# Graph attention by three sums with 0/1 fp32r patterns as stationary operands and weighted tables as moving ones

## The chip, the cores and the metric

The kernel runs on one NeuronCore of a Trainium2 chip. The metric is the device time of one execution in microseconds, as the median over the runs. One execution was also profiled; every share and duration below is of that one. The engines are called as in the profile: PE is TensorE (PEld its weight loads), DVE is VectorE, ACT is ScalarE, POOL is GpSimd, and SP issues most of the DMAs.

## The reference

Four graph layers over N = 2708 nodes with 512 features and one 0/1 adjacency matrix `adj` (about 2.4% ones, symmetric, ones on the diagonal). Each layer normalizes its input, applies a relu, and adds its result to x. Layers 0, 1 and 3 multiply the adjacency (or a part of it) by features. Layer 2, the one that changes, is attention with 8 heads of 64 outputs:

```python
Wh = jnp.einsum('nd,hdo->hno', x, W)
f1 = jnp.einsum('hno,ho->hn', Wh, a1)
f2 = jnp.einsum('hno,ho->hn', Wh, a2)
e = jax.nn.leaky_relu(f1[:, :, None] + f2[:, None, :], negative_slope=0.2)
e = jnp.where(adj[None, :, :] > 0, e, NEG_INF)
attention = jax.nn.softmax(e, axis=-1)
h_prime = jnp.einsum('hnm,hmo->hno', attention, Wh)
out = jax.nn.elu(h_prime)
```

Since leaky_relu is max(s, 0.2 s), the weight of a pair is max(exp(f1+f2), exp(0.2(f1+f2))); a factor that depends on the row alone falls out of the softmax.

## The kernel before

`fast_layers` does the four layers one after the other. Nodes are cut into NC = 22 chunks of R = 126 (the last has 62), and the chunks into six groups of 4, 4, 4, 4, 3, 3. The transposed adjacency stays in SBUF as int8 tiles `vT`, written in layer 0; `pattern(m, cs)` is its block of row chunk m and column chunks cs. The residual x lives in DRAM between the layers (x1, x2, x3).

Layers 1, 2 and 3 each begin with a dense part: `staged` runs, chunk by chunk and each stage one step behind the other, load, `norm` (statistics on DVE, a square root on ACT), `relu_T` (four PE transposes, the relu copy `hT` on ACT) and the products. Layers 0, 1 and 3 then call an aggregation: for every group and every row chunk, DVE makes a 0/1 block of fp32r (`kt`, L539 and L763) and PE multiplies it, as stationary operand, with two parts of the features (`halves`, L306), 512 columns each.

The dense part of layer 2 (`product2`) also gives f1 and f2 for each node, in `f12`; `row2` writes f1 transposed to DRAM (`rT`). After it DVE works out `bad` and a matmul the verdict that decides whether the fast path holds, and the fused weights of layer 3 are loaded. Then comes the attention, for three spans of 7, 8 and 7 column chunks, in each for eight heads: SP loads a row of rT to all partitions (`rb`), ACT takes its exponential. For each of 22 row chunks ACT multiplies it by a scalar per partition (L717), DVE takes the maximum with another scalar and multiplies with the pattern (L720), and PE multiplies with Wh as stationary operand, 65 columns wide (64 outputs and a column of ones), in fp32 with two banks of 504 or 378 moving columns (L730). An fp32 matmul is two PE instructions in the profile. `finish` transposes the result back, divides, applies the elu and adds the residual on POOL (L697).

[...]

## Time and profile before

| | |
|---|---|
| median of 3 runs (lowest, highest) | 2176.9 us (2171.16, 2180.18) |
| profiled execution: own time | 2177.88 us |
| its span, first to last instruction | 2176.0 us |
| mean granted PE clock | 0.987 |
| PE busy | 2096.1 us, 7162 instructions |
| DVE busy | 1394.2 us, 2155 instructions |
| ACT busy | 988.2 us, 1506 instructions |
| POOL busy | 245.7 us, 419 instructions |
| DMA moved | 140.65 MB, mean 65 GB/s |

The stages are told apart by the first and last PE instruction of each line:

| stage | us from the span's start |
|---|---|
| layer 0, with the fusion of layer 3's weights | 0 to 414.4 |
| layer 1, dense | 414.4 to 584.8 |
| layer 1, aggregation | 584.8 to 805.8 |
| layer 2, dense and verdict | 805.8 to 929.1 |
| layer 2, attention | 929.1 to 1787.0 |
| layer 3, dense | 1787.0 to 1948.1 |
| layer 3, aggregation | 1948.1 to 2176.0 |

A group's line names the line of the source, the engine, the operation, the tile written and those read, the shape, the count; after the bar come busy time in us and mean length of one in ns; after the second bar the idle time of the engine in front of them, with what ended it. In the timeline, instructions of one group that follow each other are merged: start, length from the first start to the last end, and the count.

### The profile page before, as it was taken

How to read it: one execution, taken by the hardware profiler on the slowest of the kernel's cores; microseconds unless marked ns; L12 is line 12 of the kernel's file. 1: busy time of each engine (PE TensorE's matmuls, PEld its weight loads, DVE VectorE, ACT ScalarE, POOL GpSimd, SP SyncE). 2: the span in 40 equal slices, each digit the busy share in tenths (PEclk: the TensorE clock that was granted, in tenths of full speed). 3: DMA queues.
4: the chain of work that ended last, by engine and by line, in shares of the span. 5: the costliest groups of instructions: out<-in, count | busy, mean ns of one | idle time of the engine just before them, and what ended most of it. 6: DMA issues, size and time to landing. Idle time of an engine off the chain costs nothing.

```text
span 2176.0 us, 21201 instructions
## 1 busy us (share of the span) xinstructions
PE 2096.1 (96%) x7162; PEld 1101.0 (51%) x7162; DVE 1394.2 (64%) x2155; ACT 988.2 (45%) x1506; POOL 245.7 (11%) x419
## 2 busy tenths in 40 slices
PE   8999998899999989799999999999999999999998
PEld 4556666544588764333333333333333334458886
DVE  5556778644455667677888787878887864323343
ACT  3456787611100002277777777767777752210000
POOL 1002323211111212300000000000010100000000
PEclk9999999999999999999999999999999999999999
DMA  7324544322311222110101110100110003211131
GB/s 241 89 76 143 147 144 143 104 68 76 103 39 39 74 68 65 37 33 26 25 25 34 54 29 28 29 19 25 31 32 25 24 12 99 68 50 58 58 112 35
DMA packets 118230, 140.65 MB, mean 65 GB/s; under 512 B 57128, under 2 KB 73748, under 8 KB 118112
## 3 DMA queue, kind: packets, MB, share of 16 engines
q1 hardware_dynamic: 80008, 103.74, 16.3%
q10 hardware_dynamic: 37528, 33.37, 5.0%
q0 software_dynamic: 576, 2.10, 0.3%
q8 instruction: 58, 0.95, 0.2%
q14 instruction: 60, 0.49, 0.1%
HBM read 103.54 MB, written 35.46 MB: 64 GB/s over the span
## 4 chain that ended last, share of the span: by engine, by line
PE 50%; ACT 3%; DMA 2%; DVE 2%; issue 1%; POOL 0%; SPq 0%; ACTq 0%; DVEq 0%; POOLq 0%
PE att L730 32%; PE acc L306 10%; PE nb_ps L165 3%; PE self_ps L165 3%; ACT t L717 2%; DMA rb<-rT 2%; DVE t L720 1%; PE out_ps L666 1%; ACT ot L663 1%; PE hT_ps L186 0%; DVE ln_st L170 0%; ACT rb L709 0%; POOL xs L697 0%; DVE x L775 0%; DVE hn L177 0%
## 5 line engine op out<-in xcount | busy, mean ns | idle before, releaser
L730 PE MATMUL att<-t,wh 126*65 126x504 f32 (+2 forms) x2112 | 832.8, 555 | 9.2 <-DVE t L720 9.2
L720 DVE SCALAR_TENSOR_TENSOR t<-t,eg,vT 126x882 f32<-126x882 f32 (+3 forms) x528 | 631.5, 1210 | 165.6 <-ACT t L717 156.4
L717 ACT ACTIVATE t<-rb,ef 126x882 f32<-126x882 f32 (+3 forms) x528 | 554.7, 1063 | 217.4 <-PE att L730 172.7
L730 PEld LDWEIGHTS att<-t,wh 126*65 126x65 f32 (+1 forms) x2112 | 288.6, 138 | 537.4 <-issue 450.0
L306 PE MATMUL acc<-halves,kt 126*126 126x512 f32 x1848 | 432.3, 395 | 0.0
L306 PEld LDWEIGHTS acc<-halves,kt 126*126 126x126 f32 x1848 | 344.0, 186 | 86.3 <-issue 1.0
L306 PE MATMUL acc<-halves,ar 126*126 126x512 f32 x924 | 254.9, 416 | 4.7 <-DVE ar L387 3.9
L306 PEld LDWEIGHTS acc<-halves,ar 126*126 126x126 f32 x924 | 166.1, 189 | 48.6 <-issue 7.0
L174 ACT ACTIVATE ln_rs<-ln_mv,eps 126x1 f32<-126x1 f32 x88 | 25.3, 294 | 306.3 <-DMA x<-x 208.7
L539 DVE SCALAR_TENSOR_TENSOR kt<-lastr,index,vT 126x504 fp32r<-126x504 int16 (+1 forms) x132 | 104.3, 798 | 83.2 <-PE acc L306 83.0
L697 POOL TENSOR_TENSOR xs<-xs,e 126x448 f32<-126x448 f32 (+3 forms) x32 | 53.6, 1686 | 822.1 <-DVE e L683 822.1
L763 DVE CAST kt<-vT 126x504 fp32r<-126x504 int8 (+1 forms) x132 | 52.7, 400 | 144.8 <-PE acc L306 140.8
L394 DVE TENSOR_TENSOR_SCAN cum<-ai,deg 126x504 int16<-126x504 int32 (+2 forms) x110 | 124.7, 1140 | 24.1 <-DMA ai<-in_adj 14.9
L404 ACT ACTIVATE sign<-cum,limit 126x504 bf16<-126x504 int16 (+3 forms) x132 | 88.5, 670 | 69.3 <-DVE cum L394 62.2
L188 ACT ACTIVATE hT<-hT_ps 128x504 f32<-128x504 f32 x88 | 51.2, 587 | 148.9 <-PE hT_ps L186 126.3
L170 DVE BATCH_NORM_STATS2 ln_st<-x 126x6 f32<-126x512 f32 x88 | 60.0, 684 | 74.3 <-DMA x<-x 67.3
L165 PE MATMUL wh_ps<-w2s,hT 128*126 128x512 f32 (+1 forms) x176 | 83.3, 617 | 9.2 <-ACT hT L188 9.2
L444 ACT CAST vT<-vT_ps 126x504 int8<-126x504 f32 (+1 forms) x132 | 70.7, 537 | 46.4 <-DVE sums L435 23.8
L389 ACT ACTIVATE ab<-ai 126x504 bf16<-126x504 int32 (+3 forms) x132 | 76.1, 579 | 18.3 <-DMA ai<-in_adj 12.9
L165 PE MATMUL nb_ps<-wn,hT 128*126 128x512 f32 x176 | 81.5, 607 | 2.6 <-ACT hT L188 2.6
L165 PE MATMUL h_ps<-w0s,hT 128*126 128x512 f32 x176 | 79.3, 593 | 0.2 <-ACT hT L188 0.2
L165 PE MATMUL nb_ps<-wfn,hT 128*126 128x512 f32 x176 | 79.3, 593 | 0.2 <-ACT hT L188 0.2
(135 smaller groups left out, 1535.8 us busy)
## 6 DMA issues: line engine op xcount, KB each, us to landing
x<-x SPq DMA_DIRECT2D x105, 252.0 KB
ai<-in_adj SPq DMA_DIRECT2D x84, 248.1 KB
x<-x ACTq DMA_DIRECT2D x63, 252.0 KB
x<-in_x SPq DMA_DIRECT2D x42, 252.0 KB
rb<-rT SPq DMA_DIRECT2D x16, 434.1 KB
s<-y ACTq DMA_DIRECT2D x21, 252.0 KB
sc<-s SPq DMA_DIRECT2D x21, 252.0 KB
out_x<-x ACTq DMA_DIRECT2D x21, 252.0 KB
```

The lines of the kernel that those rows point to most:

```text
L165: nc.tensor.matmul(po[:n], lhsT[:, f, :n], w[:, f, :], start=(f == 0), stop=(f == NF - 1))
L170: nc.vector.bn_stats(st[:n], xc[:n])
L306: nc.tensor.matmul(acc[:R], weight[:, k * R : (k + 1) * R], parts[:, i, :], start=(m == 0 and i == 0), stop=(m == NC - 1),)
L389: nc.scalar.activation(ab[:n, :gw], ai[:n, :gw], AF.Square)
L394: nc.vector.tensor_tensor_scan(cum[:n, :gw], ai[:n, :gw], ai[:n, :gw], 0.0 if g == 0 else deg[:n, m : m + 1], op0=ALU.add, op1=ALU.max,)
L404: nc.scalar.activation(sign[:n, :gw], cum[:n, :gw], AF.Sign, bias=limit[:n], scale=-1.0, accum_out=signs[:n, m, g : g + 1],)
L444: nc.scalar.copy(vT[g][:, :, m * R : (m + 1) * R], pt[:R, :K, :R])
L539: nc.vector.scalar_tensor_tensor(by_chunk(kt, cs), lastr[:, cs[0] * R : (cs[-1] + 1) * R].rearrange("p (c r) -> p c r", r=R), index[:R, m ...
L697: nc.gpsimd.tensor_tensor(xs[:n, :q], xs[:n, :q], e[:n, k : k + q], ALU.add)
L717: nc.scalar.activation(t[:n, :W], rb[:n, :W], AF.Copy, scale=ef[:n, m, hd : hd + 1])
L720: nc.vector.scalar_tensor_tensor(by_chunk(t, cs)[:n], by_chunk(t, cs)[:n], eg[:n, m, hd : hd + 1], pattern(m, cs, n), op0=ALU.max, op1=ALU ...
L730: nc.tensor.matmul(a[:O1, : hi - lo], wh[:n, m, hd, :], t[:n, lo:hi], start=(m == 0), stop=(m == NC - 1),)
```

## The change

The weight max(A, B) of a pair is A where f1 + f2 > 0 and B elsewhere. So the sum over neighbours is split into three: the sum of exp(f2) Wh over the neighbours with f2 > -f1, the sum of exp(0.2 f2) Wh over the same ones, and the sum of exp(0.2 f2) Wh over all neighbours, from which the second is taken away. The patterns hold 0 and 1 in fp32r; the weighted Wh is kept as an fp32r part and the remainder, also in fp32r.

- The dense part of layer 2 stores Wh (with its column of ones) to DRAM (`whd`). For the first pair of heads it also builds the tables: the exponentials on ACT (`tables2`), the products on POOL (`build_product`), the first part as a copy on ACT (`build_first`), the remainder on POOL (`build_second`). A table covers two row chunks and two heads; 14 buffers hold the 11 of a pair of heads and three to spare. Tables of the other pairs are built during the attention, from Wh loaded back (`load_pair`).
- The attention runs over 4 pairs of heads, 4 spans of 6, 6, 5, 5 column chunks and the 2 heads: 32 units of 22 steps. At each step DVE makes one fp32r mask (`make_mask`, five buffers, four steps ahead), and PE multiplies each 126 columns of it, as stationary operand, with 260 columns of a table. The sums over all neighbours are made once for a pair of heads: ACT casts blocks of the pattern to fp32r (`make_block`), PE multiplies them (`multiply_adj`) in between by a count (`fill`), nine steps of it at each change of unit.
- After a unit ACT copies the sums from PSUM, with a factor per row for one of them (`evict`). POOL subtracts and adds (`sum_up`), DVE takes the reciprocal and POOL multiplies (`divide`), ACT and DVE do the elu, and POOL adds the residual, loaded by SP (`load_res`), for two heads at a time (`store`).
- The verdict is worked out after the dense part of layer 3, the maxima of w2 within layer 1's aggregation.
- The pools `common` and `ps` are closed before the attention and opened again after it; they and those of the attention and layer 3 wait for reused memory tile by tile (`reuse_waits="tile"`). Several pools move to the right side of SBUF.

```diff
-    common = ctx.enter_context(tc.tile_pool(name="common", bufs=2))
-    ps = ctx.enter_context(tc.tile_pool(name="ps", bufs=8, space=PSUM))
+    def open_front():
+        nonlocal front, common, ps
+        front = ctx.enter_context(ExitStack())
+        common = front.enter_context(tc.tile_pool(name="common", bufs=2, reuse_waits="tile"))
+        ps = front.enter_context(tc.tile_pool(name="ps", bufs=8, space=PSUM, reuse_waits="tile"))
+    front = common = ps = None
+    open_front()
...
+    HP = H // 2
+    W1 = 2 * O1
+    l2 = ExitStack()
+    wk = l2.enter_context(tc.tile_pool(name="l2", bufs=1, side="right"))
+    whd = dram.tile([NC * R, H * O1], F32, name="whd")
+    scales = wk.tile([R, HP, NC, 4], F32, name="scales")
+    u = wk.tile([R, NC, H], F32, name="u")
+    def build_product(p, i, parts):
+        raw = wk.tile([R, 2, 4, O1], F32, name="raw", bufs=2)
+        for k, src in parts:
+            q = src.shape[1] // 2
+            nc.gpsimd.tensor_tensor(
+                raw[:, k : k + q].rearrange("p m (h e) o -> p (m h) e o", e=2),
+                src.unsqueeze(2).to_broadcast([R, 2 * q, 2, O1]),
+                scales[:, p, 2 * i + k : 2 * i + k + q, :]
+                .rearrange("p m (h e) -> p (m h) e", e=2)
+                .unsqueeze(3)
+                .to_broadcast([R, 2 * q, 2, O1]),
+                ALU.mult,
+            )
+        built[p, i] = raw
+    def build_first(p, i):
+        t = wk.tile([R, 2, 4, 2, O1], F32R, name="table", bufs=RING)
+        nc.scalar.copy(
+            t[:, :, :, 0, :].rearrange("p m e o -> p (m e) o"),
+            built[p, i].rearrange("p m e o -> p (m e) o"),
+        )
+        tables[p, i] = t
+    def build_second(p, i, eng):
+        t = tables[p, i]
+        v = t.rearrange("p m e q o -> p (m e) q o")
+        eng.tensor_tensor(
+            v[:, :, 1, :],
+            built.pop((p, i)).rearrange("p m e o -> p (m e) o"),
+            v[:, :, 0, :].bitcast(F32),
+            ALU.subtract,
+        )
+        tables[p, i] = t.rearrange("p m e q o -> p m (e q o)")
...
+            wh = whs[c % 4]
+            nc.scalar.copy(wh[:n, :, :O], po[:n].rearrange("p (h o) -> p h o", h=H))
+            nc.sync.dma_start(whd[c * R : (c + 1) * R, :], wh.rearrange("p h o -> p (h o)"))
...
+        def tables2(c):
+            if c % 2 == 0:
+                return
+            f2 = f12[:R, c - 1 : c + 1, H:].rearrange("p c (h e) -> p c h e", e=2)
+            for e, scale in ((slice(0, 4, 3), 1.0), (slice(1, 3), SLOPE2)):
+                nc.scalar.activation(
+                    scales[:, :, c - 1 : c + 1, e].rearrange("p h c e -> p c h e"),
+                    f2,
+                    AF.Exp,
+                    scale=scale,
+                )
+            build_product(0, c // 2, [(k, whs[(c - 1 + k) % 4][:, :2, :]) for k in range(2)])
+        def first2(c):
+            if c % 2:
+                build_first(0, c // 2)
+                build_second(0, c // 2, nc.gpsimd)
+        staged(
+            NC, *dense(x2, product2, False, [(5, row2), (5, tables2), (6, first2)])
+        )
+        nc.scalar.activation(u, f12[:R, :, :H], AF.Exp, scale=1.0 - SLOPE2)
+    front.close()
...
+    sizes2 = [6, 6, 5, 5]
+    spans = [list(range(sum(sizes2[:g]), sum(sizes2[: g + 1]))) for g in range(len(sizes2))]
+    SM = max(sizes2)
+    wide = [(p, cs) for p in range(HP) for cs in spans]
+    units = [(p, cs, e) for p, cs in wide for e in range(2)]
+    UNITS = len(units)
+    PIECE = 2
+    pieces = [
+        (t, k, cs[k : k + PIECE]) for t, (p, cs) in enumerate(wide) for k in range(0, len(cs), PIECE)
+    ]
+    blocks = [(j, g) for j in range(len(pieces)) for g in range(len(groups))]
...
+        at = stack.enter_context(tc.tile_pool(name="att", bufs=1, reuse_waits="tile"))
+        pe = stack.enter_context(tc.tile_pool(name="pe", bufs=3, space=PSUM, reuse_waits="tile"))
+        pg = stack.enter_context(tc.tile_pool(name="pg", bufs=1, space=PSUM, reuse_waits="tile"))
...
+        def make_mask(i):
+            n, m = divmod(i, NC)
+            p, cs, e = units[n]
+            q = rows(m)
+            mask[i] = at.tile([R, SM * R], F32R, name="mask", bufs=5)
+            nc.vector.scalar_tensor_tensor(
+                by_chunk(mask[i], cs)[:q],
+                by_chunk(row[n], cs)[:q],
+                f12[:q, m, H + 2 * p + e : H + 2 * p + e + 1],
+                pattern(m, cs, q),
+                op0=ALU.is_lt,
+                op1=ALU.mult,
+            )
+        def multiply(i):
+            n, m = divmod(i, NC)
+            p, cs, e = units[n]
+            q = rows(m)
+            if m == 0:
+                acc[n] = [
+                    pe.tile([P, 2, 512], F32, name="acc2") for _ in range(0, len(cs), 2)
+                ]
+            for k in range(len(cs)):
+                nc.tensor.matmul(
+                    acc[n][k // 2][:R, k % 2, : 2 * W1],
+                    mask[i][:q, k * R : (k + 1) * R],
+                    tables[p, m // 2][:q, m % 2, 2 * e * W1 : 2 * (e + 1) * W1],
+                    start=(m == 0),
+                    stop=(m == NC - 1),
+                )
+        def evict(n):
+            p, cs, e = units[n]
+            t = at.tile([R, SM, 2, 2, O1], F32, name=f"sums{e}")
+            flat = t.rearrange("p c g q o -> p c g (q o)")
+            for k, c in enumerate(cs):
+                a = acc[n][k // 2]
+                nc.scalar.activation(
+                    flat[:, k, 0],
+                    a[:R, k % 2, e * W1 : (e + 1) * W1],
+                    AF.Copy,
+                    scale=u[:, c, 2 * p + e : 2 * p + e + 1],
+                )
...
+            sums[n] = t
+        def make_block(b):
+            j, g = blocks[b]
+            cs = pieces[j][2]
+            K = len(groups[g])
+            block[b] = at.tile([R, KMAX, PIECE * R], F32R, name="block", bufs=3)
+            nc.scalar.copy(
+                block[b][:, :K, : len(cs) * R], vT[g][:, :, cs[0] * R : (cs[-1] + 1) * R]
+            )
...
+        def multiply_adj(i):
+            j, m = divmod(i, NC)
+            t, k0, cs = pieces[j]
+            p, _ = wide[t]
+            q = rows(m)
+            g, gk = where[m]
+            b = j * len(groups) + g
...
+            if m == 0:
+                accg[j] = pg.tile([P, PIECE, 512], F32, name="accg")
+            for k in range(len(cs)):
+                nc.tensor.matmul(
+                    accg[j][:R, k, : 2 * W1],
+                    block[b][:q, gk, k * R : (k + 1) * R],
+                    tables[p, m // 2][:q, m % 2, W1 : 3 * W1],
+                    start=(m == 0),
+                    stop=(m == NC - 1),
+                )
+            if m == NC - 1:
+                if k0 == 0:
+                    whole[t] = at.tile([R, SM, 2, 2, O1], F32, name="whole")
+                nc.scalar.copy(
+                    whole[t].rearrange("p c h q o -> p c (h q o)")[:, k0 : k0 + len(cs)],
+                    accg.pop(j)[:R, : len(cs), : 2 * W1],
+                )
...
+        def sum_up(t):
+            p, cs = wide[t]
+            y[t] = at.tile([R, SM, 2, O1], F32, name="y2")
+            parts[t] = [(k, min(3, len(cs) - k)) for k in range(0, len(cs), 3)]
+            for e in range(2):
+                s = sums[2 * t + e].rearrange("p c g q o -> p c g (q o)")
+                w = whole[t].rearrange("p c h q o -> p c h (q o)")
+                for k, q in parts[t]:
+                    v = slice(k, k + q)
+                    nc.gpsimd.tensor_tensor(s[:, v, 1], w[:, v, e], s[:, v, 1], ALU.subtract)
+            for e in range(2):
+                s = sums[2 * t + e].rearrange("p c g q o -> p c g (q o)")
+                for k, q in parts[t]:
+                    v = slice(k, k + q)
+                    nc.gpsimd.tensor_tensor(s[:, v, 0], s[:, v, 0], s[:, v, 1], ALU.add)
+            for e in range(2):
+                s = sums.pop(2 * t + e)
+                for k, q in parts[t]:
+                    v = slice(k, k + q)
+                    nc.gpsimd.tensor_tensor(y[t][:, v, e], s[:, v, 0, 0], s[:, v, 0, 1], ALU.add)
...
+        def divide(t):
+            p, cs = wide[t]
+            K = len(cs)
+            rs = at.tile([R, SM, 2, 1], F32, name="rs2", bufs=2)
+            nc.vector.tensor_scalar(rs[:, :K], y[t][:, :K, :, O:], TINY, None, op0=ALU.max)
+            nc.vector.reciprocal(rs[:, :K], rs[:, :K])
+            for k, q in parts[t]:
+                v = slice(k, k + q)
+                nc.gpsimd.tensor_tensor(
+                    y[t][:, v, :, :O],
+                    y[t][:, v, :, :O],
+                    rs[:, v].to_broadcast([R, q, 2, O]),
+                    ALU.mult,
+                )
+        def elu(t, part):
+            k, q = parts[t][part]
+            v = y[t][:, k : k + q, :, :O]
+            z = at.tile([R, 3, 2, O], F32, name="z2")
+            th = at.tile([R, 3, 2, O], F32, name="th2")
+            nc.scalar.activation(z[:, :q], v, AF.Relu, scale=-1.0)
+            nc.scalar.activation(v, v, AF.Relu)
+            nc.scalar.activation(th[:, :q], z[:, :q], AF.Tanh, scale=-0.5)
+            nc.scalar.activation(z[:, :q], z[:, :q], AF.Exp, scale=-1.0)
+            exps[t, k] = z, th
+        def store(t, part):
+            p, cs = wide[t]
+            k, q = parts[t][part]
+            z, th = exps.pop((t, k))
+            x = xs.pop((t, k))
+            nc.vector.scalar_tensor_tensor(
+                z[:, :q], z[:, :q], 1.0, th[:, :q], op0=ALU.add, op1=ALU.mult
+            )
+            for i, w, n, dst in rows_of(x3, p, cs, k, q):
+                v = x[:n, i : i + w].rearrange("p c (h o) -> p c h o", h=2)
+                nc.gpsimd.tensor_tensor(v, v, y[t][:n, k + i : k + i + w, :, :O], ALU.add)
+                nc.gpsimd.tensor_tensor(v, v, z[:n, i : i + w], ALU.add)
+                nc.scalar.dma_start(dst, x[:n, i : i + w])
...
+        for n in range(1, UNITS):
+            at_step(max(0, (n - 1) * NC + 3), load_rows, n)
+        for p in range(1, HP):
+            e0 = (2 * len(spans) * p - 1) * NC
+            spare = RING - NC // 2
+            for i in range(NC // 2):
+                free = e0 + 2 * (i - spare) + 2 if i >= spare else e0 - 4 * (spare - i)
+                at_step(free - 12, load_pair, p, i)
+                at_step(free - 3, product_of, p, i)
+                at_step(free + 1, build_first, p, i)
+                at_step(
+                    free + 2,
+                    build_second,
+                    p,
+                    i,
+                    nc.vector if i >= spare and (i - spare) % 2 else nc.gpsimd,
+                )
+        STEPS = UNITS * NC
+        for t in range(len(wide)):
+            e0 = 2 * NC * (t + 1)
+            for lag, fn, args in (
+                (1, sum_up, ()),
+                (10, load_res, ()),
+                (18, divide, ()),
+                (24, elu, (0,)),
+                (27, store, (0,)),
+                (28, elu, (1,)),
+                (31, store, (1,)),
+            ):
+                at_step(e0 + lag, fn, t, *args)
+        BURST, AHEAD, GAP = 9, 2, 2
+        per_unit = len(pieces) * NC // UNITS
...
+        LEAD = 4
+        load_rows(0)
+        for i in range(LEAD):
+            make_mask(i)
+        fill(0, BURST + AHEAD)
+        for i in range(STEPS):
+            for fn, args in plan.pop(i, ()):
+                fn(*args)
+            if i + LEAD < STEPS:
+                make_mask(i + LEAD)
+            multiply(i)
+            n, m = divmod(i, NC)
+            base = per_unit * n + AHEAD + BURST
+            fill(i, base + (per_unit - BURST) * (m + 1) // NC)
+            if m == NC - 1:
+                evict(n)
+                fill(i + GAP, base + per_unit)
+    l2.close()
+    open_front()
...
-                for m in range(NC):
-                    n = rows(m)
-                    t = wk.tile([R, WM], F32, name="t2", bufs=5)
-                    nc.scalar.activation(
-                        t[:n, :W], rb[:n, :W], AF.Copy, scale=ef[:n, m, hd : hd + 1]
-                    )
-                    nc.vector.scalar_tensor_tensor(
-                        by_chunk(t, cs)[:n],
-                        by_chunk(t, cs)[:n],
-                        eg[:n, m, hd : hd + 1],
-                        pattern(m, cs, n),
-                        op0=ALU.max,
-                        op1=ALU.mult,
-                    )
-                    for i, a in enumerate(acc):
-                        lo, hi = i * HALF * R, min(W, (i + 1) * HALF * R)
-                        nc.tensor.matmul(
-                            a[:O1, : hi - lo],
-                            wh[:n, m, hd, :],
-                            t[:n, lo:hi],
-                            start=(m == 0),
-                            stop=(m == NC - 1),
-                        )
-                finish(cs, hd, acc)
-        l2w.close()
...
```

## The prediction

> **What bounds the kernel now.** I read the page first, then the windows cut at the stages, then the groups by form, last the timeline around the GpSimd instructions of the attention.
>
> ```profile
> PE 2096.1 (96%) x7162; PEld 1101.0 (51%) x7162; DVE 1394.2 (64%) x2155; ACT 988.2 (45%) x1506; POOL 245.7 (11%) x419
> ...
> L730 PE MATMUL att<-t,wh 126*65 126x504 f32 (+2 forms) x2112 | 832.8, 555 | 9.2 <-DVE t L720 9.2
> ```
>
> TensorE is busy nearly throughout. The windows say what it is busy with (columns: stretch, its length, then PE, PEld, DVE, ACT, POOL busy, granted clock, DMA share, GB/s):
>
> ```profile
> 805.80:929.10 123.30, 95.47 (x289) 44.35 (x289) 79.81 (x183) 35.65 (x92) 39.30 (x26) 0.92 0.23 69
> 929.10:1787.00 857.90, 848.57 (x2290) 301.32 (x2291) 690.98 (x763) 622.12 (x656) 52.38 (x30) 0.99 0.10 27
> 1787.00:1948.10 161.10, 160.85 (x441) 74.77 (x440) 54.96 (x115) 32.52 (x62) 1.78 (x3) 1.00 0.23 74
> ```
>
> The middle line is the attention that is replaced: 857.9 us, bound by the fp32 matmuls, with POOL nearly idle. The line above is the dense part of layer 2, with 28 us of idle PE; the one below the dense part of layer 3.
>
> **TensorE after.** New matmuls have 126x126 fp32r weights and 260 moving columns. There are 32 units x 22 row chunks x 5.5 column chunks = 3872 for the masks and 48 pieces x 22 rows, 2 chunks each less the odd ones, = 1936 for the adjacency: 5808. Nearest rows:
>
> ```profile
> 600.00:700.00 100.00, 100.00 (x432) 80.13 (x431) 55.20 (x71) 0.00 (x0) 13.88 (x8) 1.00 0.14 42
> ```
>
> ```profile
> 414.30:416.80 2.50, 2.50 (x22) 2.26 (x21) 1.00 0.18 67
> ```
>
> ```profile
> L306 PEld LDWEIGHTS acc<-halves,kt 126*126 126x126 f32 x1848 | 344.0, 186 | 86.3 <-issue 1.0 <-DVE kt L539 0.8
> ```
>
> ```profile
> 1791.62 3.60 PE L165 MATMUL self_ps<-wfs,hT 128*126 128x512 f32 x8
> ```
>
> The first: fp32r with 512 columns and a weight load each, 432 in 100 us, 231.5 ns apiece. In proportion, 260 columns take 117.6 ns. The last: eight fp32 instructions in 3.60 us, the last record 0.59, so 430 ns each; if an fp32r matmul streams at twice that rate, 512 columns need 215 ns and 16.5 ns is fixed, and 260 columns take 109 + 16.5 = 125.7. Bounds: below, 117.6 (683 us in all); above, the weight load's record of 186 ns, if loads cannot overlap one another (1080 us). The second line, 22 transposes with 126-column loads in 2.50 us, 114 ns each under load records of 136 ns, shows that such records do overlap. I take 125.7 ns: **730 us**, 1.04 us for each of the 704 mask steps.
>
> [...]
>
> **VectorE after.** It makes 704 masks, half of 756 columns, half of 630, with the form of L720: fp32 tile, per-row scalar, int8 pattern. Here are such instructions with and without a GpSimd instruction beside them (timeline of DVE; two, three or two in a row):
>
> ```profile
> 1107.89 3.06 DVE L720 SCALAR_TENSOR_TENSOR t<-t,eg,vT 126x882 f32<-126x882 f32 x2
> 1111.53 3.23 DVE L720 SCALAR_TENSOR_TENSOR t<-t,eg,vT 126x882 f32<-126x882 f32 x3 [0.58 <-ACT t L717]
> ...
> 1330.09 3.45 DVE L720 SCALAR_TENSOR_TENSOR t<-t,eg,vT 126x1008 f32<-126x1008 f32 x2
> ...
> 1360.32 2.45 DVE L720 SCALAR_TENSOR_TENSOR t<-t,eg,vT 126x1008 f32<-126x1008 f32 x2 [1.06 <-ACT t L717]
> ...
> 1558.07 2.92 DVE L720 SCALAR_TENSOR_TENSOR t<-t,eg,vT 126x882 f32<-126x882 f32 x2
> 1562.60 4.28 DVE L720 SCALAR_TENSOR_TENSOR t<-t,eg,vT 126x882 f32<-126x882 f32 x4 [1.61 <-ACT t L717]
> ```
>
> Undisturbed, one more of 882 columns takes (3.23 - 1.14)/2 = 1.045 us, one of 1008 takes 2.45 - 1.27 = 1.18: 1.07 ns a column. So 0.91 us for 756 and 0.775 for 630: 352 x 1.685 = **593 us**. Two of 882 alone take 1.14 + 1.045 = 2.19. Beside it DVE does 12 table subtractions (0.6 us, L227's row), 32 products of the elu (0.33 to 0.47, from L683) and 32 tiny ones (0.08): 24 us. Together 617.
>
> **GpSimd after, and what it does to VectorE.** The POOL timeline at the same places:
>
> ```profile
> 1108.11 1.90 POOL L697 TENSOR_TENSOR xs<-xs,e 126x448 f32<-126x448 f32 x1 [31.90 <-DVE e L683]
> ...
> 1330.31 2.17 POOL L697 TENSOR_TENSOR xs<-xs,e 126x512 f32<-126x512 f32 x1 [33.48 <-DVE e L683]
> ```
>
> With one GpSimd add of 448 elements between them, two VectorE instructions take 3.06 us for 2.19; with 512, 3.45 for 2.45; with 384, 2.92 for 2.19. The two engines take turns: each GpSimd add of n elements costs VectorE 2.11 ns x n - 0.08 us. Before, 32 such adds did no harm, as DVE had 167 us of slack. The change queues some 350 in this stage: `sum_up` (192 adds, 57,200 elements), `divide` (32; 11,264), `store` (72; 22,528), tables (54 of 520 elements, 28,080), 119,000 elements in all: 251 - 28 = **223 us** that VectorE must stand aside. Masks and POOL's work together need 617 + 223 = 840 us, more than TensorE's 730.
>
> [...] The add of 448 ran 0.99 us after VectorE's end but cost 0.87, as the next instruction's start lies under it. [...]
>
> That the strided and broadcast adds cost what L697's plain ones do is not shown. Below, nothing suggests less than half (112 us); above, I allow one and a half times (335). I take the plain rate.
>
> **The attention's time.** Smoothed perfectly it is 840 us. If no step could borrow from the next, 350 steps with a GpSimd instruction cost 0.84 + 0.64 us, 354 without it TensorE's 1.04, and the 24 come on top: 909. Five mask buffers let DVE run four steps ahead, so a run of six adds is half absorbed; I take the middle, **875**.
>
> ScalarE: 288 block casts (L717: 1.13 us for 1008 columns, 0.92 for 756) 282 us; evictions about 100 (L663: 0.56 for 504 columns); elu and tables 80. Some 465 of 875, hidden. The new SP loads (33 for tables, 36 of x for 32, 32 rows for 24) go where DMA is at 0.10; if late, a table would hold TensorE.
>
> **Edges.** Dense part of layer 2: ACT gains 14 table switches between Exp and Sqrt of 1.28 us (L174's ACT_TABLE_LOAD), 22 Exp and 11 casts, all ahead of the hT copy that PE waits for; ACT is 35.65 busy in 123.30, so most is covered: 0 to 18, I take 8. The 22 stores of Wh on SP stand before x loads that are prefetched several chunks ahead: nothing; late, they would show as waits of DVE on x. Start of the attention: from 914 to 929 PE works 2 us; the verdict moves to layer 3, rows can be loaded earlier, and adjacency matmuls need no mask: 0 to -13, I take -10. End: x3 loads now wait for the attention's buffers, where PE had 0.25 us of idle: 0 to 8, I take 5. Moved maxima of w2, verdict: nothing, beside DVE at 60%; uncovered, about 5 us.
>
> Sum against the profiled execution (span 2176.0, own time 2177.9): 2177.9 - 857.9 + 875 + 8 - 10 + 5 = 2198. It lies 1.0 above the median of 2176.9: **2197 us**.
>
> **Rivals.**
> - *TensorE bound, faster.* GpSimd's adds fall where VectorE waits anyway, or the fp32r-writing masks do not take turns with them. For it: DVE alone needs 617, below 730. Against: L539, which writes fp32r too, has a mean of 842 ns at 504 columns, GpSimd's adds beside it, where undisturbed ones take 0.73 us (timeline at 632 us). Attention 730 + 35 = 765, in all 2087. Chance 0.22.
> - *Queued waits, slower.* DVE's first instruction of `divide` stands in the built program's queue behind only six masks of the next unit, and waits for the last six sums on POOL, which wait for ACT's eviction: 2.9 + 4.4 us less the four masks in hand (3.4) is 4 us, 16 times, about 58 more: 2255. It decides when the waits find no mask in reserve. Chance 0.13.
> - *Weight loads exposed, slower.* 186 ns a matmul, 1080 us: 2403. It decides when matmul spacing exceeds 145 ns (840/5808). The 114 ns row speaks against it. Chance 0.09.
> - *Two engines by turns*, my forecast, 840 to 909 in the attention, 2162 to 2231: 0.56.
>
> **How the numbers follow.** A measurement of this kernel can tell about 0.5%, 10.9 us: 2166 to 2188 is the same. Of the forecast's 0.56, 0.04 lie below, 0.15 within and 0.37 above. Faster 0.22 + 0.04 = 0.26, same 0.15, slower 0.59. The range, 2080 to 2310, leaves out the exposed loads and half of the TensorE-bound case, about 2 in 10; its upper end is the sum with one and a half times POOL's cost, 2197 + 112. The forecast's own range is 2162 to 2231.
>
> **What would show it.** Right: in the attention window DVE busy near its whole length with masks of mean well above 1.0 us, POOL at 35% or more, PE idle before masks (released by DVE's `mask`). Wrong: masks at 1.0 and 0.87 us beside a busy POOL (turns do not happen), PE busy throughout with 126 ns a matmul (TensorE bound), or PE spacing near 190.

## The result, and the profile after

The changed kernel took 2231.0 us (median of 4 runs, 2230.2 to 2231.4) beside 2175.9 us for the kernel before (4 runs): a ratio of 1.0253, 95% interval 1.0231 to 1.0275. It is slower by 55 us, where 20 had been forecast. The span of its profiled execution is 2229.4 us.

From the page, the busy line and three groups:

```profile
PE 2044.8 (92%) x10682; PEld 1553.5 (70%) x10682; DVE 1473.8 (66%) x2191; ACT 803.3 (36%) x1665; POOL 679.0 (30%) x773
...
L741 DVE SCALAR_TENSOR_TENSOR mask<-rb,f,vT 126x756 fp32r<-126x756 f32 (+1 forms) x704 | 723.3, 1092 | 72.6 <-PE acc L759 71.7
L759 PE MATMUL acc<-table,mask 126*126 126x260 f32 (+1 forms) x3872 | 610.3, 296 | 49.4 <-DVE mask L741 48.9
...
L841 POOL TENSOR_TENSOR sums<-whole,sums 126x390 f32<-126x390 f32 x64 | 84.1, 1319 | 305.8 <-ACT whole L824 305.8
```

VectorE's masks and TensorE's matmuls now wait for each other, and GpSimd's busy time has grown from 245.7 to 679.0 us. The windows of the changed kernel (stretch, length, busy time of PE, PEld, DVE, ACT, POOL, granted clock, DMA share, GB/s), cut at the same places as those of before, with layer 0 ahead of them:

```profile
0.00:419.30 419.30, 387.15 (x1794) 251.45 (x1795) 282.02 (x592) 261.12 (x623) 88.86 (x315) 0.98 0.46 136
810.90:934.50 123.60, 95.78 (x287) 44.42 (x287) 89.69 (x180) 58.13 (x134) 66.67 (x62) 0.90 0.36 113
934.50:1818.80 884.30, 793.60 (x5808) 751.58 (x5808) 751.54 (x774) 409.82 (x754) 447.69 (x335) 0.94 0.10 30
1818.80:2001.10 182.30, 163.46 (x443) 76.11 (x442) 62.53 (x139) 38.70 (x83) 11.30 (x18) 0.94 0.25 79
```

| stage | before | after | change | forecast |
|---|---|---|---|---|
| layer 0 | 414.4 | 419.3 | +4.9 | 0 |
| layer 1, both parts | 391.4 | 391.6 | +0.2 | 0 |
| layer 2, dense, to the attention's first matmul | 123.3 | 123.6 | +0.3 | -2 |
| attention | 857.9 | 884.3 | +26.4 | +17 |
| layer 3, dense | 161.1 | 182.3 | +21.2 | +5 |
| layer 3, aggregation | 227.9 | 228.3 | +0.4 | 0 |
| span | 2176.0 | 2229.4 | +53.4 | +20 |

No engine is full in the attention: VectorE is busy 751.5 of 884.3 us. Counted in the trace, VectorE or GpSimd or both are busy in 843 of the 884 us: GpSimd works in 92 of the 133 us in which VectorE stands, and in 41 neither does. The waits of that stage (engine, line, releaser: total, times, longest):

```profile
DVE mask L741 <- PE acc L759: 71.7, 39, 8.0
...
DVE rs L875 <- POOL y L851: 53.3, 12, 6.3
PE acc L759 <- DVE mask L741: 48.9, 61, 2.8
```

VectorE waits 53.3 us in the division (L875) for GpSimd's last sums, with GpSimd busy in 51.6 of them, and 71.7 us for mask buffers that TensorE has not released; in 36.8 of these GpSimd stands too. At the border to layer 3, TensorE's timeline and then VectorE's:

```profile
1818.05 0.76 PE L759 MATMUL acc<-table,mask 62*126 62x260 f32 x5
1837.65 1.91 PE L196 MATMUL hT_ps<-ident,hn 126*128 126x126 f32 x8 [18.84 <-DVE hn L187]
```

```profile
1824.55 0.17 DVE L875 TENSOR_SCALAR rs<-y 126x10 f32<-126x10 f32 x1 [6.80 <-POOL y L851]
...
1828.05 0.56 DVE L903 SCALAR_TENSOR_TENSOR z<-z,th 126x384 f32<-126x384 f32 x1 [3.08 <-ACT z L895]
1831.86 0.43 DVE L903 SCALAR_TENSOR_TENSOR z<-z,th 126x256 f32<-126x256 f32 x1 [3.25 <-ACT z L895]
1832.20 1.60 DVE L1050 CAST kt<-vT 126x504 fp32r<-126x504 int8 x3
1833.72 0.68 DVE L180 BATCH_NORM_STATS2 ln_st<-x 126x6 f32<-126x512 f32 x1
```

TensorE stands for 18.84 us. Layer 3's loads of x went out at 1818.73 (SyncE's timeline), but the first norm on VectorE (L180) comes only at 1833.72, behind the last span pair's division, both halves of its ELU and three casts. In the kernel before, the first three of these norms (its L177) had run at 1228 to 1233 us, and the same place cost TensorE 0.25 us:

```profile
1786.81 1.03 PE L186 MATMUL hT_ps<-ident,hn 126*128 126x126 f32 x8
1788.09 3.70 PE L165 MATMUL nb_ps<-wfn,hT 128*126 128x512 f32 x8 [0.25 <-ACT hT L188]
```

After the stand TensorE is also slow for a while in the changed kernel: the eight products from 1839.40 on took 5.34 us, at a granted clock of 0.69 in that stretch, and the eight after them 3.60.

### The profile page after: what moved, and what is told of

Read it like the earlier page. It is cut to its first block, busy times and chain, and to the rows that moved or that the text cites. A ratio compares the mean times of both kernels' runs of the same rounds, so it can differ in the third digit from the quotient of the medians.

```text
span 2229.4 us, 29457 instructions
## 1 busy us (share of the span) xinstructions
PE 2044.8 (92%) x10682; PEld 1553.5 (70%) x10682; DVE 1473.8 (66%) x2191; ACT 803.3 (36%) x1665; POOL 679.0 (30%) x773
## 4 chain that ended last, share of the span: by engine, by line
PE 65%; POOL 13%; DVE 7%; ACT 6%; issue 5%; DMA 3%; SPq 0%; ACTq 0%; POOLq 0%; DVEq 0%
PE acc L316 25%; PE acc L759 13%; PE nb_ps L175 7%; PE accg L814 7%; PE self_ps L175 3%; PE line_ps L175 3%; PE h_ps L175 3%; POOL sums L841 3%; POOL sums L846 3%; DVE mask L741 2%; POOL raw L606 2%; PE hT_ps L196 1%; DMA ai<-in_adj 1%; POOL table L628 1%; ACT block L794 1%
## 5 line engine op out<-in xcount | busy, mean ns | idle before, releaser
L741 DVE SCALAR_TENSOR_TENSOR mask<-rb,f,vT 126x756 fp32r<-126x756 f32 (+1 forms) x704 | 723.3, 1092 | 72.6 <-PE acc L759 71.7
L759 PE MATMUL acc<-table,mask 126*126 126x260 f32 (+1 forms) x3872 | 610.3, 296 | 49.4 <-DVE mask L741 48.9
L759 PEld LDWEIGHTS acc<-table,mask 126*126 126x126 f32 (+1 forms) x3872 | 531.9, 196 | 75.9 <-DVE mask L741 67.8
L814 PE MATMUL accg<-table,block 126*126 126x260 f32 (+1 forms) x1936 | 363.3, 297 | 45.3 <-ACT whole L824 33.4
L814 PEld LDWEIGHTS accg<-table,block 126*126 126x126 f32 (+1 forms) x1936 | 289.3, 195 | 60.9 <-ACT whole L824 37.9
L794 ACT CAST block<-vT 126x1008 fp32r<-126x1008 int8 (+3 forms) x288 | 255.5, 921 | 205.9 <-PE accg L814 185.2
L841 POOL TENSOR_TENSOR sums<-whole,sums 126x390 f32<-126x390 f32 x64 | 84.1, 1319 | 305.8 <-ACT whole L824 305.8
L180 DVE BATCH_NORM_STATS2 ln_st<-x 126x6 f32<-126x512 f32 x88 | 60.0, 684 | 84.9 <-DMA x<-x 71.8
L198 ACT ACTIVATE hT<-hT_ps 128x504 f32<-128x504 f32 x88 | 51.2, 585 | 163.1 <-PE hT_ps L196 161.8
L412 POOL CAST deg<-cum 126x1 f32<-126x1 int16 (+1 forms) x132 | 41.0, 311 | 226.2 <-DVE cum L404 206.6
L414 ACT ACTIVATE sign<-cum,limit 126x504 bf16<-126x504 int16 (+3 forms) x132 | 88.5, 670 | 58.3 <-DVE cum L404 53.3
L568 POOL TENSOR_TENSOR x<-x,y 126x512 f32<-126x512 f32 (+1 forms) x22 | 36.3, 1657 | 187.4 <-DVE y L565 93.3
```

Source lines behind the costliest of these rows:

```text
L414: nc.scalar.activation(sign[:n, :gw], cum[:n, :gw], AF.Sign, bias=limit[:n], scale=-1.0, accum_out=signs[:n, m, g : g + 1],)
L741: nc.vector.scalar_tensor_tensor(by_chunk(mask[i], cs)[:q], by_chunk(row[n], cs)[:q], f12[:q, m, H + 2 * p + e : H + 2 * p + e + 1], patte ...
L759: nc.tensor.matmul(acc[n][k // 2][:R, k % 2, : 2 * W1], mask[i][:q, k * R : (k + 1) * R], tables[p, m // 2][:q, m % 2, 2 * e * W1 : 2 * (e ...
L794: nc.scalar.copy(block[b][:, :K, : len(cs) * R], vT[g][:, :, cs[0] * R : (cs[-1] + 1) * R])
L814: nc.tensor.matmul(accg[j][:R, k, : 2 * W1], block[b][:q, gk, k * R : (k + 1) * R], tables[p, m // 2][:q, m % 2, W1 : 3 * W1], start=(m == 0),
L841: nc.gpsimd.tensor_tensor(s[:, v, 1], w[:, v, e], s[:, v, 1], ALU.subtract)
```

## The experiments

Three questions: what the 26 us in the attention are, what the 21 at the border are, and what layer 0's 5 are. Each stage is read from that run's own profile, since layer 0 alone ended at 419.2 to 426.1 us over 11 of the profiles.

**1. The additions on VectorE.** L841, L846, L851:

```diff
-nc.gpsimd.tensor_tensor(s[:, v, 1], w[:, v, e], s[:, v, 1], ALU.subtract)
+nc.vector.tensor_tensor(s[:, v, 1], w[:, v, e], s[:, v, 1], ALU.subtract)
 ... (L846 and L851 alike)
```

> The 192 additions that gather each span pair's sums (L841, L846, L851) go from GpSimd to VectorE; nothing else is changed. Theory A (the two engines take turns at SBUF, and VectorE's reciprocal waits in its queue for GpSimd's sums): VectorE gets about 72 us of additions (192 x 0.37 us by the rows of its own additions of that size), loses about 63 us of lengthened masks (84 + 155 us of GpSimd's additions gone) and the 53 us of waits at L875; the attention goes from 884 to about 840 us, the whole to about 2187 us. Theory B (TensorE's own pace, with stretches of matmuls at 215 ns, sets the attention): VectorE's waits move to L741 and the attention stays at 875 to 890 us, the whole within 10 us of 2231. Theory C (VectorE is already the bound with its masks): the attention grows by up to 72 us, to 2290 us.

2178.0 us, ratio 1.0012 (1.0003 to 1.0022). The window of the attention:

```profile
936.10:1767.40 831.30, 777.30 (x5808) 742.52 (x5808) 775.50 (x957) 405.48 (x754) 248.67 (x151) 0.95 0.11 32
```

53 us less, although VectorE has 183 instructions more: its busy time rose by 24 us, and its idle time fell from 133 to 56. TensorE's 5808 matmuls are the same, so it was not the bound. Theory A holds, but two parts of it (turns and queue) left together.

**2. Two of the three rounds of additions left out.**

```diff
-nc.gpsimd.tensor_tensor(s[:, v, 1], w[:, v, e], s[:, v, 1], ALU.subtract)
-nc.gpsimd.tensor_tensor(s[:, v, 0], s[:, v, 0], s[:, v, 1], ALU.add)
 ... (with their loops)
```

> Two of the three rounds of GpSimd's additions (L841, L846: the adjacency sums less the masked ones, and the two joined) are left out, so y holds the first sums alone; the third (L851) stays. Theory A (turns at SBUF and queued waits on GpSimd's sums): 128 of the 192 additions go, some 160 us of GpSimd's time; VectorE gains about 45 us of shorter masks and most of the 53 us of waits at L875; the attention comes to about 790 to 810 us, the whole to about 2145. Theory B (TensorE's pace is the bound): the attention stays at 870 us or more, the whole above 2215.

2133.5 us, ratio 0.9804 (0.9788 to 0.9821).

```profile
935.30:1725.90 790.60, 750.88 (x5808) 721.54 (x5808) 720.35 (x774) 409.87 (x754) 290.26 (x213) 0.98 0.12 33
```

The attention falls by 93.7 us. The 128 additions have 45,760 elements; by the prediction's price of 2.11 ns x n - 0.08 us they cost VectorE 96.6 - 10.2 = 86 us. The 93.7 are not all of that kind: VectorE's busy time fell by 31 us and its idle time by 62. The time in which VectorE or GpSimd is busy fell by 81, from 843 to 763 us, and that is the figure to hold beside the 86.

**3. The division's lags.**

```diff
-                (18, divide, ()),
-                (24, elu, (0,)),
+                (26, divide, ()),
+                (32, elu, (0,)),
 ... (and the three after it by 8)
```

> The division of a span pair (VectorE's L875 and L876 with GpSimd's L879) and the steps behind it stand eight masks later in the order: lags 26, 32, 35, 36 and 39 in place of 18, 24, 27, 28 and 31. The work is the same, GpSimd's additions included. Theory A1 (VectorE's queue: the reciprocal stands before masks while GpSimd still sums): the 53 us of waits at L875 all but vanish and the attention falls from 884 to 830 to 845 us, the whole to about 2185. Theory A2 (the turns at SBUF alone carry the loss): the masks beside GpSimd stay as long as they are and the attention stays at 875 us or more, the whole above 2220. In between (855 to 865 us, the whole near 2205) each carries about half.

2226.8 us, ratio 1.0217 (1.0201 to 1.0232); attention 876.0 us; L875 still waits 47.7 us. The test missed its aim: counted in the trace, the reciprocal still stands 6 or 7 masks into the next unit in 12 of the first 15 pairs, as in the changed kernel. In both kernels it stands ahead of the place that the text gives it (lags of 18 and of 26 steps), and the later place did not hold it back.

**4. The division tied behind a mask.**

```diff
+with tc.issue_after(newest[0].ins):   # the newest mask
     nc.vector.tensor_scalar(rs[:, :K], y[t][:, :K, :, O:], TINY, None, op0=ALU.max)
     nc.vector.reciprocal(rs[:, :K], rs[:, :K])
```

> The reciprocal of a span pair (L875, L876 of the kernel after) is tied behind the newest mask of its step, so that it stands 23 masks into the next unit on VectorE in all of the first 15 pairs, where the lags alone had left 12 of them at 6 or 7 masks. The work is the same and GpSimd's additions stay on GpSimd. Theory A1 (the queued wait costs the 53 us): the waits at L875 go and the attention falls from 884 to 830 to 845 us, the whole to 2180 to 2195. Theory A2 (the wait is a symptom: TensorE and VectorE are held by GpSimd's turns, and the masks would wait elsewhere): less than 15 us of the 53 come back, the attention stays at 870 us or more, the whole above 2215.

2233.7 us, ratio 1.0277 (1.0259 to 1.0295). VectorE's waits in the attention (lines have moved by two to three):

```profile
DVE mask L743 <- PE acc L761: 78.9, 44, 7.4
DVE z L906 <- ACT z L898: 33.7, 12, 2.8
```

```profile
936.00:1818.00 882.00, 791.50 (x5808) 757.11 (x5808) 767.70 (x774) 409.84 (x754) 507.42 (x335) 0.93 0.10 30
```

The 53.3 us at the reciprocal are gone, and the attention is 2.3 us shorter. VectorE's busy time rose by 16, its waits for ScalarE by 28, for TensorE by 7. GpSimd's busy time rose from 447.7 to 507.4 us with the same 335 instructions, and the masks' mean from 1092 to 1115 ns: additions beside which VectorE had waited (51.6 of the 53.3 us) now stand beside masks. The time in which VectorE or GpSimd is busy is 830 us, for 843 in the changed kernel. So the queued wait was mostly time that GpSimd's work needed anyway: theory A2. The test is not a clean one, though: 28 of the 53 us came back as another queued wait, that of VectorE's ELU product (L906) for ScalarE, whose steps had stayed where they were. What the stage takes with neither wait and GpSimd's additions where they are was not run.

**5. The last span pair's tail left out.** In `divide`, `elu` and `store`, for the last pair only; its rows of x go out unchanged, on SyncE's queue in place of ScalarE's:

```diff
+if t == len(wide) - 1 and fn in (divide, elu, store):
+    fn, args = (residual, args) if fn is store else (None, ())
 ... (a step without a function is passed over)
```

> The last span pair's division, ELU and addition of the residual are left out: its rows of the input are copied unchanged to the layer's output. Theory A (the head of layer 3 stands in VectorE's queue behind that pair's chain through GpSimd, VectorE, GpSimd, ScalarE, VectorE, GpSimd and a store): TensorE's idle time between the attention and layer 3 falls from 18.8 us to 5 to 8 us, the whole by 11 to 14 us. Theory B (the loads of x, issued when the attention ends, and the norms of the first chunk set it): the idle time stays above 15 us and the whole at 2228 or more.

2220.6 us, ratio 1.0203 (1.0181 to 1.0226). TensorE at the border:

```profile
1819.08 0.76 PE L759 MATMUL acc<-table,mask 62*126 62x260 f32 x5
1829.11 1.91 PE L196 MATMUL hT_ps<-ident,hn 126*128 126x126 f32 x8 [9.27 <-DVE hn L187]
```

9.3 us in place of 18.8: half of it, a little less than expected. That the rest is loads and norms that start only when the attention ends is tried in 7 to 9.

**6. Pools that wait as wholes.** `reuse_waits="tile"` taken from every pool.

> The pools wait as whole pools again: the tile-by-tile waits are taken from all of them, the places and sizes stay. Theory A (what the layers' borders cost is which bytes are reused, and the tile waits soften that): layer 3's loads of x wait for the last store of the attention (15 us after its last matmul) and TensorE's idle time before layer 3 grows from 18.8 us to some 30 to 35; the attention's start waits for the last of layer 2, 2 to 5 us more; the whole comes to about 2247 (2240 to 2255). Theory B (tile waits bring nothing, the queues set the borders): the whole stays at 2231, within 4 us. Layer 0's first adjacency loads stay at 55 us in both.

2243.7 us, ratio 1.0299 (1.0283 to 1.0315). The loads of x go out 17.0 us after the attention's end (1841.00 against 1824.0) in place of 0.1 before it, and TensorE's first product of layer 3 comes after 28.0 us in place of 20.6; TensorE stands 26.2 us, less than the 30 to 35 expected. The tile waits of the change are worth some 13 us in all; they soften a border that the reopened pools make.

**7. Two chunks of layer 3 made ready early.**

```diff
-RING = 14
+RING = 13
 ...
+early = ctx.enter_context(tc.tile_pool(name="early", bufs=1))
 ...
+for c in range(2):
+    at_step(650, early_load, c)   # x3 rows into early tiles
+    at_step(660, early_norm, c)   # normalised in place
```

> Two tiles for the rows of layer 3's first two chunks are kept through the attention (paid by a table ring of 13 in place of 14); their loads and norms are put 54 and 44 masks before the attention's end. Theory A (the border costs 18.8 us because the front's bytes are the attention's, so that x arrives and is normalised only after its end, behind the last pair's chain): TensorE's idle time at the border falls to 3 to 8 us and the whole by 10 to 15 us, to 2216 to 2221, if the shorter ring costs nothing. Theory B (the accumulators or the chain of stores hold layer 3): the idle time stays above 15 us and the whole at 2228 or more.

2231.4 us, ratio 1.0251 (1.0236 to 1.0266): nothing in the whole. In its profile the stage from the attention's end to the end of layer 3's dense part fell from 182.3 to 178.6 us (and layer 0 happened to end at 423.1 in place of 419.3). ScalarE's timeline says why it is so little:

```profile
1835.40 0.32 ACTq L910 DMA_DIRECT2D x<-xs  x1
...
1838.59 0.83 ACTq L910 DMA_DIRECT2D x<-xs  x2
1839.47 1.07 ACT L198 ACTIVATE hT<-hT_ps 128x504 f32<-128x504 f32 x2 [2.08 <-POOL xs L909]
```

TensorE made its transposes 0.7 us after the attention, and then their copy (L198) stood behind the last pair's ELU and stores in ScalarE's queue until 1839.5. Removing one wait only showed the next.

**8. A tile of its own for that copy.** `hT` of the two early chunks in the `early` pool; `kt3` with 2 buffers for 3.

> The two early chunks of the run before it, and their transposed copy (L198's output) also has a tile of its own for both chunks in turn, paid by two in place of three casted blocks in layer 3's aggregation. Theory A (bytes: the copy waited because its tile lay on bytes of the last pair's tiles): ScalarE makes the first copy before the last pair's ELU, TensorE starts layer 3's products about 2 us after its early transposes, works 7 us, and stands again until the second copy behind the stores; the stage from the attention's end to the end of layer 3's dense part falls from 178.6 to 170 to 174 us, the whole by 5 to 8 us against the two early chunks alone. Theory B (ScalarE's queue order is fixed by the steps, not the bytes): the first product still starts 15 us after the attention's end and the stage stays at 178 or more.

2231.3 us, ratio 1.0246 (1.0231 to 1.0260). The first copy had waited for its bytes; TensorE's timeline:

```profile
1829.91 3.70 PE L175 MATMUL nb_ps<-wfn,early_hT 128*126 128x512 f32 x8 [0.64 <-ACT early_hT L198]
1833.45 3.60 PE L175 MATMUL self_ps<-wfs,early_hT 128*126 128x512 f32 x8
1848.12 1.10 PE L196 MATMUL hT_ps<-ident,hn 126*128 126x126 f32 x4 [11.07 <-DVE hn L187]
```

The first product comes 2.4 us after the attention's end (1827.5), works 7 us, and TensorE stands 11 us more. The stage is 175.8 us, above the 170 to 174 expected; the whole shows nothing, as layer 0 ended at 426.1 in this profile.

**9. Both edits, 5 and 7.** The last pair's division, ELU and residual are left out here too.

> The two early chunks of layer 3, and the last span pair's division, ELU and addition of the residual left out (its rows of the input are copied unchanged), both at once. Theory A (the border is made of two things, the front's bytes and the last pair's chain ahead in the queues): with both gone TensorE's first product of layer 3 starts 3 to 6 us after the attention's end, where it was 20.6 us after it in the kernel after, 11 without the chain and 15.7 with the early chunks; the stage to the end of layer 3's dense part falls from 182 to 164 to 168 us, the whole to 2211 to 2217. Theory B (the norms and loads of the third and later chunks set the stage): the stage stays at 172 us, as without the chain alone.

2218.7 us, ratio 1.0192 (1.0177 to 1.0207).

```profile
1822.75 0.77 PE L759 MATMUL acc<-table,mask 62*126 62x260 f32 x5
1824.17 1.08 PE L196 MATMUL hT_ps<-ident,early 126*128 126x126 f32 x8 [0.65 <-ACT sums L782]
1825.88 3.70 PE L175 MATMUL nb_ps<-wfn,hT 128*126 128x512 f32 x8 [0.63 <-ACT hT L198]
```

| | first product after the attention's end | stage |
|---|---|---|
| before | 1.1 us | 161.1 us |
| after | 20.6 | 182.3 |
| without the chain (5) | 11.0 | 172.4 |
| early chunks (7) | 15.7 | 178.6 |
| both (9) | 2.4 | 162.6 |

The border is settled: the chain alone gives 9.9 us, the early chunks alone 3.7, both 19.7 of the 21.2. Each of the two hides behind the other. The stage holds TensorE's slow stretch behind its stand too: the first eight products took 5.34 us in the changed kernel and 3.70 here.

**10. Layer 0's pool.** First only to the right side, `tc.tile_pool(name="l0", bufs=2, side="right")`:

> Layer 0's work pool goes to the right side of SBUF, off the bytes that the preparation's pools release; nothing else is changed. Theory A (the place of the pool makes the first adjacency loads wait until 55 us, and with that TensorE's first work): layer 0 comes back from 419.3 to about 414.4 us, the whole falls by about 5 us. Theory B (the waits by tile, not the place, are the cause): layer 0 stays at 419 us and the whole at 2231.

2229.4 us, ratio 1.0250 (1.0233 to 1.0268); layer 0 at 419.2 us. The first adjacency loads still went out at 55.8 us, so this run decided nothing about the place. Then with the ring on the left and `wc` single:

> Layer 0's work pool on the right side beside the patterns, the ring on the left, and the preparation's largest tile single: layer 0's adjacency tiles now lie on bytes that no tile of the preparation uses, which the move to the right alone had not reached. Theory A (the place of the pool): the first adjacency loads go out at about 15 us in place of 55, TensorE's first aggregation matmul starts near 53 us in place of 59, layer 0 ends at 414 to 415 us in place of 419.3; the whole falls by 4 to 6 us to about 2226. Theory B (something else holds layer 0, such as the loads' order in SyncE's queue): layer 0 stays at 418 to 420 us, the whole at 2229 to 2231.

2232.1 us, ratio 1.0247 (1.0231 to 1.0262). The first adjacency loads go out at 15.2 us in place of 55.3, the first aggregation matmul at 54.1 in place of 59.2: the place of the pool, on bytes that no earlier tile holds, ends that wait. But layer 0 ends at 417.4, and the whole gains nothing that can be told. Over all profiles, layer 0 ended at 419.2 to 426.1 us (11 kernels, mean 421.2) without this edit and at 411.8 to 421.4 (4 kernels, mean 417.6) with it. The means differ by 3.6 us, less than one profile differs from the next, so what the place is worth in the whole is not shown.

**11. Joined versions.** The first: edits 1 and 10, the division's products by ScalarE, the last pair's residual on VectorE and its stores by SyncE.

> Joined: the 192 additions on VectorE, layer 0's pool on clear bytes, the division's products by ScalarE (176 products of 126x64 with a scale of one value per row) in place of GpSimd (30 products), the last span pair's residual additions on VectorE and its stores on SyncE's queue. Theory A (turns and queued waits on GpSimd): from the 831 us that the additions alone gave, 66 us less of GpSimd beside the masks bring another 15 to 25 us, attention 806 to 816; layer 0 gives 5 us, the end 2 to 4; the whole about 2150 us (2142 to 2160). Theory B (ScalarE's queue then holds the blocks and evictions that TensorE waits for; 176 products by 0.3 us are 53 us more there): the attention stays at 830 us or more and the whole at 2168 to 2185.

2187.0 us, ratio 1.0033 (1.0021 to 1.0046), slower than edit 1 alone: a miss, as theory B had it. The attention took 837.4 us, and layer 3's loads of x stood behind the stores in SyncE's queue, 1787.9 for an attention that ended at 1774.5. The second: edits 1, 7 and 10, the division's products and the last pair's residual on VectorE, the tables' second parts all on GpSimd.

> Joined: the 192 additions, the division's 30 products and the last pair's residual additions on VectorE, all second parts of the tables on GpSimd, layer 0's pool on clear bytes, and the two early chunks of layer 3. VectorE gains 30 x 0.5 us of products and loses 12 x 1.4 us of second parts; GpSimd loses 66 us and gains 18. Theory A (turns at SBUF): 48 us less of GpSimd beside the masks, by the 0.3 to 0.45 us that each of its microseconds cost, bring 14 to 22 us: attention 810 to 818 us; the border gives 10 to 15, layer 0 about 2; the whole 2145 to 2155 us. Theory B (VectorE at 93% is the bound and what is put on it counts in full): the attention stays at 828 us or more, the whole at 2162 to 2170.

2162.9 us, ratio 0.9943 (0.9930 to 0.9957). The attention:

```profile
928.40:1751.90 823.50, 763.96 (x5808) 729.26 (x5808) 782.13 (x983) 409.27 (x758) 198.77 (x133) 0.96 0.12 33
```

VectorE is busy 95% of it. The gain in the attention is 8 us where 14 to 22 were expected: theory A's direction, nearer to B's size. With edit 8 as well:

> The second joined kernel with the early copy's own tile added. Theory A (bytes): TensorE's first product of layer 3 starts about 3 us after the attention's end in place of 12, the stage to the end of layer 3's dense part falls from 175.1 to 167 to 170 us, the whole from 2162.9 to about 2157 (2152 to 2160). Theory B: the stage stays at 174 us or more and the whole at 2161 or more.

2160.6 us, ratio 0.9921 (0.9908 to 0.9933): faster than the kernel before by 0.8% and than the changed one by 3%. The step from the second joined version, 2.3 us, lies within the spread of the runs; the stage after the attention fell from 175.0 to 172.0.

## Why the prediction was right or wrong

**The direction and the mechanism were right.** *Two engines by turns*: masks have a mean of 1092 ns, GpSimd is busy 51% of the stage, TensorE waits 48.9 us for masks. VectorE is busy 85%, not near the whole length as the text had it. What the sum stands for is the time in which VectorE or GpSimd is busy: 617 + 223 = 840 us forecast, 843 counted. Some of GpSimd's work falls not into longer masks but into waits of VectorE, at the reciprocal above all.

**TensorE, 125.7 ns a matmul:** the starts of the matmul records in the attention lie 121 ns apart in the median. The forecast's split of the 231.5 ns into a rate, twice that of the fp32 rows, and a fixed part was the author's estimate; no run separates the two. TensorE is not the bound: with the same matmuls the stage took 790.6 us in experiment 2. The TensorE-bound and the exposed-load rivals fall (the latter needed a spacing above 145 ns).

**Masks, 593 us:** 15 masks of 756 columns in a row took 13.38 us where GpSimd was idle (timeline at 1029.67 us of the changed kernel) and ten of 630 took 7.93 us (at 1818.55 us of experiment 8), so 0.885 and 0.785 us from start to start: 352 x 1.67 = 588 us.

**GpSimd's price, 223 us:** 86 us by the price for the additions that experiment 2 left out; the time in which either engine works fell by 81, the stage by 94, waits included.

**The attention, 875 us:** measured 884.3, inside the 840 to 909. Of the 267 us above the floor of 617, 134 are VectorE's lengthened work and 133 its idle time. The 35 us put on top of 840 stood for steps that cannot borrow from each other; 41 were counted with both engines still, 36.8 of them VectorE's waits for mask buffers. That the middle of two bounds came within 9 us is in part luck. What the 9 us are was not tested; the last section has a candidate.

**The rival of queued waits** had its 58 us (3.9 us for each of the 15 pairs that have a next unit; the text counts 16) named rightly in place and nearly in size (53.3, at 12 of the 15), but as a charge on top. GpSimd worked in 51.6 of the 53.3 us, so they are in the 840 already. Experiment 4 took them away and won 2.3 us, but it put another queued wait of 28 us in; how much of the loss is waiting and how much is turns stays open in that part.

**The step that failed is the edges, above all "End: ... I take 5".** It measured 21.2. It priced only that the loads wait for the attention's buffers. It did not follow what was queued ahead of layer 3's norms and copies on VectorE and ScalarE, namely the last pair's sums, division, ELU and stores, one engine after another with nothing beside them, and that norms which had been done during the attention now begin after it. Experiments 5, 7 and 9 show these two, and that they make 19.7 of the 21.2 us together. Of the 21.2 us, 18.6 are TensorE's longer stand; most of the rest is the slow stretch behind it, which the prediction left out as well (5.34 us for eight products in place of 3.70 before). Layer 0 had no term; its profile moved by 4.9 us, less than the 7 us by which that stage differs among kernels that have the same layer 0. Of the 33 us between the forecast and the measured span, 16 are the border, 9 the attention, 5 layer 0 and 2 the start of layer 2.

## What to carry to other kernels

GpSimd's additions beside a stream of two-input VectorE instructions cost this stage some 2 ns an element (81 to 94 us for 45,760), partly as longer instructions and partly as waits: add the two engines' times before asking which of them waits. Moving one wait gave 2 us, moving the work 53. Where a pool is closed and opened again at a stage's border, follow the last group's chain through every queue, stores included, and ask of each first step of the next stage both which bytes it waits for and what stands ahead of it; curing one of the two shows the other (9.9 and 3.7 us alone, 19.7 together). A lag in the emission order was not a place in VectorE's queue (6 or 7 masks into the unit with a lag of 18 and with one of 26): read the built order before calling an edit a test.

## What the runs showed that was not expected

At each of the three changes of the head pair one of GpSimd's additions stood for 16.1 us or more; the longest of all its other records in the attention took 4.23. VectorE and then GpSimd in the changed kernel:

```profile
1144.90 5.61 DVE L741 SCALAR_TENSOR_TENSOR mask<-rb,f,vT 126x630 fp32r<-126x630 f32 x4
1150.44 0.68 DVE L628 TENSOR_TENSOR table<-raw,table 126x520 fp32r<-126x520 f32 x1
1151.05 17.67 DVE L741 SCALAR_TENSOR_TENSOR mask<-rb,f,vT 126x756 fp32r<-126x756 f32 x18
1176.72 1.02 DVE L741 SCALAR_TENSOR_TENSOR mask<-rb,f,vT 126x756 fp32r<-126x756 f32 x1 [8.00 <-PE acc L759]
```

```profile
1144.51 2.98 POOL L606 TENSOR_TENSOR raw<-whp,scales 126x520 f32<-126x520 f32 x2
...
1148.74 1.10 POOL L846 TENSOR_TENSOR sums<-sums 126x260 f32<-126x260 f32 x1
1149.92 16.15 POOL L851 TENSOR_TENSOR y<-sums 126x130 f32<-126x130 f32 x1
1166.03 1.89 POOL L628 TENSOR_TENSOR table<-raw,table 126x520 fp32r<-126x520 f32 x1
```

Beside GpSimd operations of 520 and 260 elements, four masks took 5.61 us, 1.4 us each for 0.785 alone. Then 18 masks ran in a row, 0.98 us each, and an addition of 130 elements stood from 1149.92 until the seventeenth of them had begun, 16.15 us; the shortest of its form took 0.41. After the row VectorE waited 8.0 us for TensorE. The same happened at 1378.74 (16.14 us) and, with an addition of 260 elements, at 1606.17 (16.39 us); in experiment 1 the longest such stand was 7.5 us. Why an addition stood so long in these three places and not elsewhere stays open, and its cost was not tried by itself.
